# A two-layer graph attention kernel: the last element's finishes cut into 13 pieces without GpSimd's additions, two maxima per beat, and its predecessor's layer 1 at 1.3 steps per beat

## The chip, the cores and the metric

The kernel runs on one core of one Trainium2 chip. The metric is device time in microseconds, of one execution. Engines are named as the profile names them: PE is TensorE's matmul, PEld its weight load, DVE is VectorE, ACT is ScalarE, POOL is GpSimd, SP is SyncE, whose queue issues the DMAs.

## What is computed

There are B = 8 elements of N = 2048 nodes with F = 256 features, and one adjacency matrix for all. Layer 0 is attention with 4 heads, whose softmax is taken over chunks of 256 keys separately; layer 1 is a graph attention layer. Each has a residual and a layer norm.

```
# layer 0
scores = clip(q @ k.T / 8, -10, 10);  scores = where(mask == 0, -10, scores)
attn = softmax(scores, within each of 8 chunks of 256 keys)
y = layernorm(sum over chunks(attn @ v) @ Wo.T + bo + x) * gamma + beta
x = layernorm(x + y)
# layer 1
Wh = x @ W;  s_i = Wh @ a1;  s_j = Wh @ a2
e = leaky_relu(s_i[:, None] + s_j[None, :], 0.2), -inf without an edge
x = layernorm(x + elu(softmax(e) @ Wh))
```

## The kernel before, in words

**Tiles.** Queries go in blocks of IB = 512 (NIB = 4 per element), keys in tiles of 128 (NT = 16) for layer 1 and chunks of 256 (NCH = 8) for layer 0. Everything is fp32, but for the masks.

**Beats.** The order of instructions on each engine is written out by hand: the program emits them in beats. There are 512 beats with scores (8 elements x 4 blocks x 16 key tiles), then a tail of beats without, until the queues of work are empty. Elements and beats are counted from 0 here. Beside the scores, a beat carries layer-1 steps of an earlier element, and one stage of each generator in two lists, `ahead` (the preludes of layer 1) and `fins` (the finishes of blocks). `begin_beat` adds a rate to a credit, and each whole credit starts a layer-1 step: RATE is 1.5 while scores of elements 0 to 6 are made, LAST_RATE (L717) is 1.1 while those of element 7 are, which are the beats that do layer 1 of element 6; in the tail it is 1.0.

**A layer-1 step** (`Step`, 16 per block) makes one key tile's weights for 512 queries in four instructions over four stages: `low` (L642, ACT, 128x512), `leaky` (L646, DVE), `edges` (L651, DVE, with the mask), `weights` (L655, ACT, exponential), and then `product`, four matmuls into PSUM (L674; for the last element L689, with a column of ones that gives the row sums). For elements 0 to 6 GpSimd adds up the weights (L664), whose column sums are the row sums. The tiles w have five buffers.

**The finish of a layer-1 block** (`fin1`, L586) is a generator: it loads the residual hr; divides by the row sums (`divided`, L613, four ACT instructions; for the last element it is called in `product` at once, after two reciprocals, L704); takes the exponential (L601, ACT, 128x1024); the ELU (L603, DVE, 128x1024); adds hr (L604, GpSimd, 128x1024); then statistics (`stats`, L316 and L317, four times each, DVE; L321; and a power -0.5 on GpSimd, L322), `normalize` (L327 on DVE, then four ACT scalings, L329), and stores 512 KB. The finish of a block is emitted in the beats of the next block's steps.

**The finish of a layer-0 block** (`fin`, L342) projects the context (L357), adds, takes statistics, normalizes, multiplies by gamma and adds the residual on GpSimd (L369, L370), takes statistics again, normalizes, stores to h_d, transposes (L382).

**The prelude of the last element** (`last_prelude`, L516). Layer 1 needs for each query the maximum over its neighbours' s_j. `half_max` (L437, one DVE instruction of 128x1024) does one query tile against one half of the keys: 32 in all, `half(it, hf)`. First halves (16) need the far masks in fb tiles, which have two buffers and are loaded one by one, each when a maximum has freed one. One such maximum goes per beat until the last block of layer 0 is finished ("hT"); what is left then is done at once. Masks of the second halves are held in eight tiles loaded together in the third tail beat (L560, 4 MB); the second halves need a row of s_j (L420) that comes out of the last layer-0 block.

**The tail**, in beats: 512 to 520 end layer 0 of the last block; 521 has the remaining first halves and the first four second halves; in 522 to 532 element 6's layer 1 ends; the last element's four blocks of 16 steps follow, each with the finish of the block before; then the last finish alone, to beat 601.

Of the kernel before, what the change touches and what calls it, by code (L numbers as in the profile page):

```python
# [9 lines left out]
F32 = mybir.dt.float32  # L10
# [9 lines left out]
P = 128  # L20
# [8 lines left out]
def tile_adj_attention__then__gat(  # L29
# [312 lines left out]
    def fin(b, ib, ctxT):  # L342


        xt = one.tile([P, TPB, F], F32, tag="x", name=f"x{b}_{ib}")
        nc.sync.dma_start(out=xt, in_=x[b, ts(ib, IB), :].rearrange("(t p) f -> p t f", p=P))
        yield
        y = one.tile([P, TPB, F], F32, tag="y", name=f"y{b}_{ib}")
        nc.gpsimd.tensor_add(y, xt, bc_rows(bo_bc))
        nc.gpsimd.tensor_add(xt, xt, bc_rows(beta_bc))  # L350
        while (b, ib) not in ctx_done or ctx_done[b, ib] == beat:
            yield
        for t2 in range(TPB // 2):
# [12 lines left out]
        yield  # L366
        normalize(y, mv, rstd, f"a{b}_{ib}")
        yield
        nc.gpsimd.tensor_mul(y, y, bc_rows(gamma_bc))  # L369
        nc.gpsimd.tensor_add(y, y, xt)  # L370
        yield
        mv, rstd = yield from stats(y, f"b{b}_{ib}")
        yield
        normalize(y, mv, rstd, f"b{b}_{ib}")
        nc.sync.dma_start(out=h_d[b, ib], in_=y)
        fin_near[b] += 1
        yield
# [138 lines left out]
    def last_prelude(b):  # L516

        st = states[b]  # L520
        wh, rows = [None] * NIB, [None] * 2
        halves = [slice(0, HT), slice(HT, NT)]
        sj = None
        for ib in range(NIB - 1):

            while fin_near[b] <= ib or beat < 2 * total - 12 + 4 * ib:
                yield
            ht = load_hT(b, ib)
            yield
# [12 lines left out]
        m2 = one.tile([P, NIB, 2, TPB], F32, tag="m2l", name=f"m2{b}")  # L542
        firsts = list(range(NT))
        held = None

        def half(it, hf):
            fb = fbs.pop(0) if hf == 0 else held[it // 2][:, ts(it % 2, HN)]
            half_max(rows[hf], fb, m2[:, it // TPB, hf, it % TPB : it % TPB + 1])
            if hf == 0:
                fb_load()  # L550

        while "hT" not in st:
            if firsts:
# [12 lines left out]
        nc.vector.memset(wh[-1][:, :, F : F + 1], 1.0)  # L566
        rows[1] = one.tile([P, HN], F32, tag="v1", name=f"sj_row{b}_1")
        key_rows(b, sj, rows[1], halves[1])
        st["wh"], st["sj"] = wh, sj
        yield  # L570
        while firsts:
            half(firsts.pop(0), 0)
        for ib in range(NIB):
            for t in range(TPB):
                half(ib * TPB + t, 1)
                if ib:
                    yield
            less_max(sj, ib, m2[:, ib], f"{b}_{ib}")
            ab_d = query_rows(m2[:, ib], f"{b}_{ib}")
            yield  # L580

            while blocks_done < b * NIB + ib - 1:
                yield
            st["ab"][ib] = (beat + 1, query_bc(ab_d, f"{b}_{ib}"))

    def fin1(b, ib, hx, acc):  # L586

        hr = one.tile([P, TPB, F], F32, tag="hr", name=f"hr{b}_{ib}")
        nc.sync.dma_start(out=hr, in_=h_d[b, ib])
        yield  # L590


        if acc is not None:
            pr = ps_m.tile([P, TPB], F32, tag="m", name=f"pr{b}_{ib}")
            for t in range(TPB):
                nc.tensor.matmul(pr[:, t : t + 1], acc[:, ts(t, P)], ones[:, 0:1], start=True, stop=True)
            r = two.tile([P, TPB], F32, tag="r1", name=f"r1{b}_{ib}")
            nc.vector.reciprocal(r, pr)
            divided(hx, [hx[:, t, :] for t in range(TPB)], r)
# [3 lines left out]
        nc.vector.scalar_tensor_tensor(hx, ex, 1.0, hx, ALU.min, ALU.max)  # L603
        nc.gpsimd.tensor_add(hx, hx, hr)  # L604
# [4 lines left out]
        nc.sync.dma_start(out=out[b, ts(ib, IB), :].rearrange("(t p) f -> p t f", p=P), in_=hx)  # L609

    def divided(hx, us, r):
        for t in range(TPB):
            nc.scalar.activation(hx[:, t, :], us[t], AF.Identity, bias=ones[:, 0:1], scale=r[:, t : t + 1])  # L613

    states = [{"ab": {}} for _ in range(B)]
    total = B * NIB * NCH
# [15 lines left out]
    class Step:  # L632
# [33 lines left out]
        def product(self):  # L666
# [28 lines left out]
                    )  # L695
            if last:
                blocks_done += 1
                hx = one.tile([P, TPB, F], F32, tag="hx", name=f"hx{self.name}")
# [7 lines left out]
                fins.append(fin1(k["b"], k["ib"], hx, k.get("acc")))  # L706

# [43 lines left out]
    def end_beat():  # L751

        nonlocal weighted
        if beat < 2 * NIB * NCH:
            for fn in agenda.pop(beat, []):
                fn()
        for s in weighted:
            s.product()
        weighted = []
        for gens in (ahead, fins) if beat < 2 * total else (fins, ahead):  # L760
            for g in list(gens):
                if next(g, g) is g:
                    gens.remove(g)
        for fn in agenda.pop(beat, []):
            fn()
# [178 lines left out]
```

## Time and profile before

| | |
|---|---|
| Time, median of 3 runs | 4405.71 us (4405.65 to 4411.56) |
| Profiled execution | 4405.8 us, its span 4404.0 us |
| Mean granted clock of TensorE | 0.979 |
| Busy: PE, PEld | 4064.3 us (92%), 1911.1 us (43%) |
| Busy: DVE, ACT, POOL | 3424.3 (78%), 2567.6 (58%), 1775.2 (40%) |
| L646, leaky, 128x512 | 512 times, mean 1145 ns; 966 ns after 4100 us |
| L651, edges, 128x512 | 512 times, mean 937 ns; 863 ns after 4100 us |
| L437, one maximum with fb, 128x1024 | 240 times, mean 1628 ns |
| L604, residual addition, 128x1024 | 32 times, mean 2856 ns |

A line of the timeline gives start, duration, engine, source line, operation, out<-in, shapes and count; brackets at its end hold the idle time of the engine before it and what ended it. A row of a table by stretches gives the stretch, its length, and each engine's busy time in it with the number of instructions, then the granted clock (1.00 is full), the share of the DMA engines and GB/s. Busy time of PE is of pipelined matmuls, and their ends are modelled.

### The profile page before, as it was taken

How to read it: one execution, taken by the hardware profiler on the slowest of the kernel's cores; microseconds unless marked ns; L12 is line 12 of the kernel's file. 1: busy time of each engine (PE TensorE's matmuls, PEld its weight loads, DVE VectorE, ACT ScalarE, POOL GpSimd, SP SyncE). 2: the span in 40 equal slices, each digit the busy share in tenths (PEclk: the TensorE clock that was granted, in tenths of full speed). 3: DMA queues.
4: the chain of work that ended last, by engine and by line, in shares of the span. 5: the costliest groups of instructions: out<-in, count | busy, mean ns of one | idle time of the engine just before them, and what ended most of it. 6: DMA issues, size and time to landing. Idle time of an engine off the chain costs nothing. (4 is left out here: it accounts for less than half of the span.)

```text
span 4404.0 us, 61164 instructions
## 1 busy us (share of the span) xinstructions
PE 4064.3 (92%) x23053; PEld 1911.1 (43%) x23053; DVE 3424.3 (78%) x4506; ACT 2567.6 (58%) x3846; POOL 1775.2 (40%) x906
## 2 busy tenths in 40 slices
PE   8889999999899999999899998999989999899667
PEld 3223334454344534454344543445434454344355
DVE  5876489965898669976699767996589965897786
ACT  5655456665566556666566665666556665565455
POOL 0222235543455334444245442554335543344421
PEclk9999999999999999999999999999999999999888
DMA  5554232222322233321333223222232222332311
GB/s 165 172 173 147 71 114 85 83 73 87 101 90 80 64 107 102 100 75 50 106 100 97 73 79 101 87 90 78 71 109 90 82 74 85 102 100 71 132 58 48
DMA packets 257625, 415.63 MB, mean 94 GB/s; under 512 B 85424, under 2 KB 120496, under 8 KB 256432
## 3 DMA queue, kind: packets, MB, share of 16 engines
q1 hardware_dynamic: 257328, 411.71, 30.2%
q8 instruction: 181, 2.97, 0.3%
q14 instruction: 116, 0.95, 0.1%
HBM read 340.66 MB, written 68.88 MB: 93 GB/s over the span
## 5 line engine op out<-in xcount | busy, mean ns | idle before, releaser
L821 ACT ACTIVATE e<-sc 128x1024 f32<-128x1024 f32 x1024 | 1034.3, 1020 | 1048.2 <-DVE sc L818 1004.8
L818 DVE SCALAR_TENSOR_TENSOR sc<-sc,mk 128x1024 f32<-128x1024 f32 x1024 | 1206.8, 1223 | 528.0 <-PE sc L808 342.3
L808 PE MATMUL sc<-qT,kT 64*128 64x512 f32 x4096 | 1059.5, 632 | 91.7 <-ACT e L821 91.5
L873 POOL TENSOR_TENSOR ctxT<-ctxT,un 128x1024 f32<-128x1024 f32 x224 | 567.4, 2533 | 1135.1 <-DVE un L872 1021.7
L837 PE MATMUL u<-e,v 128*32 128x512 f32 x8192 | 981.1, 597 | 0.0
L674 PE MATMUL us<-wh,w 128*128 128x256 f32 x3584 | 876.8, 394 | 67.7 <-ACT w L655 50.0
L674 PEld LDWEIGHTS us<-wh,w 128*128 128x128 f32 x3584 | 666.5, 193 | 408.9 <-ACT w L655 99.6
L664 POOL TENSOR_TENSOR acc<-acc,w 128x512 f32<-128x512 f32 x392 | 601.9, 1535 | 553.4 <-ACT w L655 535.0
L808 PEld LDWEIGHTS sc<-qT,kT 64*128 64x128 f32 x4096 | 346.2, 188 | 616.8 <-ACT e L821 286.9
L646 DVE SCALAR_TENSOR_TENSOR w<-ab,sj,w 128x512 f32<-128x512 f32 x512 | 576.1, 1145 | 16.4 <-ACT w L642 16.2
L837 PEld LDWEIGHTS u<-e,v 128*32 128x32 f32 x8192 | 240.7, 110 | 660.5 <-issue 545.9
L651 DVE TENSOR_TENSOR w<-w,mk 128x512 f32<-128x512 f32 x512 | 469.5, 937 | 33.7 <-DMA mk<-mask 30.8
L837 PE MATMUL u<-e,ones 128*32 128x512 f32 x4096 | 495.1, 601 | 0.0
L437 DVE CUSTOM_DVE_ANT_0 fb<-sj_row,fb 128x1024 bf16<-128x1024 f32 x240 | 388.7, 1628 | 7.8 <-DMA fb<-far 7.7
L642 ACT ACTIVATE w<-ab,sj 128x512 f32<-128x512 f32 x512 | 353.3, 715 | 19.9 <-PE us L689 12.7
L655 ACT ACTIVATE w<-w 128x512 f32<-128x512 f32 x512 | 309.3, 628 | 71.5 <-DVE w L651 70.4
L845 ACT COPY un<-u 128x512 f32<-128x512 f32 x512 | 300.6, 587 | 66.9 <-PE u L837 58.2
L872 DVE TENSOR_TENSOR un<-un,r 128x1024 f32<-128x1024 f32 x224 | 280.5, 1252 | 44.1 <-DMA r<-rd 39.0
L837 PEld LDWEIGHTS u<-e,ones 128*32 128x32 f32 x4096 | 107.6, 110 | 352.7 <-issue 301.2
L859 DVE RECIPROCAL dc<-dc 128x16 f32<-128x16 f32 x256 | 63.8, 249 | 147.7 <-DMA dc<-ds 132.0
L604 POOL TENSOR_TENSOR hx<-hx,hr 128x1024 f32<-128x1024 f32 x32 | 91.4, 2856 | 175.2 <-DVE hx L603 175.2
L689 PE MATMUL us<-wh,w 128*128 128x257 f32 x512 | 127.5, 412 | 30.3 <-ACT w L655 30.3
(100 smaller groups left out, 3135.3 us busy)
## 6 DMA issues: line engine op xcount, KB each, us to landing
r<-rd SPq DMA_DIRECT2D x256, 256.0 KB
mk<-mask SPq DMA_DIRECT2D x120, 512.0 KB
fb<-far SPq DMA_DIRECT2D x240, 256.0 KB
xT_k<-in_xT_dram SPq DMA_DIRECT2D x32, 512.0 KB
raw<-in_adjT_dram SPq DMA_DIRECT2D x32, 512.0 KB
rawf<-in_adj_dram SPq DMA_DIRECT2D x32, 512.0 KB
x<-in_x_dram SPq DMA_DIRECT2D x32, 512.0 KB
h_d<-y SPq DMA_DIRECT2D x32, 512.0 KB
```

The source lines that it names most:

```text
L437: nc.vector.tensor_tensor_reduce(out=fb, in0=row, in1=fb, scale=1.0, scalar=2 * FAR * 0.999, op0=ALU.add, op1=ALU.max, accum_out=dst,)
L642: nc.scalar.activation(self.w, k["ab"][:, 1, :], AF.Identity, bias=k["sj"][:, 1, c : c + 1])
L646: nc.vector.scalar_tensor_tensor(self.w, k["ab"][:, 0, :], k["sj"][:, 0, c : c + 1], self.w, ALU.add, ALU.max)
L651: nc.vector.tensor_tensor(self.w, self.w, self.k["mks"][self.c // HT][:, self.c % HT, :], ALU.min)
L655: nc.scalar.activation(self.w, self.w, AF.Exp)
L664: nc.gpsimd.tensor_add(k["acc"], k["acc"], self.w)
L674: nc.tensor.matmul(k["us"][:, t, :], self.w[:, ts(t, P)], k["wh"][c // TPB][:, c % TPB, 0:F], start=(first and t % 2 == 0), stop=last, ski ...
L808: nc.tensor.matmul(sc[:, h, :], kTs[b][c // TPB][h * D : (h + 1) * D, hp, ts(c % TPB, P)], qT[h * D : (h + 1) * D, hp, :], start=True, sto ...
L818: nc.vector.scalar_tensor_tensor(scs[hp], scs[hp], -CLIP, cap, ALU.max, ALU.min)
L821: nc.scalar.activation(e, scs[hp], AF.Exp)
L837: nc.tensor.matmul(m[h * DH : (h + 1) * DH, :], prev["v"][pc // TPB][:, pc % TPB, f0 : f0 + DH] if part < 2 else ones[:, 0:DH], prev["es"] ...
L873: nc.gpsimd.tensor_add(p["ctxT"], p["ctxT"], p["un"])
```

## The change

- LAST_RATE is 1.3 in place of 1.1.
- In the tail, two first-half maxima are emitted per beat in place of one, as long as there are any; the agenda (the scaling of layer-0 contexts) runs at the front of the beat's end there, too.
- The layer-0 finish of the very last block multiplies by gamma and adds the residual on DVE.
- For the last element, `fin1` is replaced by `fin1_last`. Of the four divisions, two go to DVE. The finish of blocks 0, 1, 2 has 13 pieces, one per beat: two exponentials of half the block, two ELUs, two additions on DVE, four tiles of statistics, the spread (with the power on GpSimd), two pairs of scalings, then the store. The finish of block 3 is emitted in one go, half after half, each with its own spread and store.
- Blocks 1 and 3 of the last element use the buffer of y for hx.

```diff
@@ in fin
-        nc.gpsimd.tensor_mul(y, y, bc_rows(gamma_bc))
-        nc.gpsimd.tensor_add(y, y, xt)
+        engine = nc.vector if (b, ib) == (B - 1, NIB - 1) else nc.gpsimd
+        engine.tensor_mul(y, y, bc_rows(gamma_bc))
+        engine.tensor_add(y, y, xt)
@@ in last_prelude
-            if firsts:
-                half(firsts.pop(0), 0)
+            for it in firsts[: 2 if beat > 2 * total else 1]:
+                half(it, 0)
+                firsts.remove(it)
@@ new
+    def fin1_last(b, ib, hx):
+        hr = one.tile([P, TPB, F], F32, tag="hr", name=f"hr{b}_{ib}")
+        nc.sync.dma_start(out=hr, in_=h_d[b, ib])
...
+        def exponential(r):
+            nc.scalar.activation(ex[:, r, :], hx[:, r, :], AF.Exp, bias=shifts[:, 1:2])
+        def elu(r):
+            nc.vector.scalar_tensor_tensor(hx[:, r, :], ex[:, r, :], 1.0, hx[:, r, :], ALU.min, ALU.max)
+        def add(r):
+            nc.vector.tensor_add(hx[:, r, :], hx[:, r, :], hr[:, r, :])
+        def tile_stats(t):
+            nc.vector.bn_stats(st[:, t, :], hx[:, t, :])
+            nc.vector.bn_aggr(mv[:, t, :], st[:, t, :])
+        def spread_of(r):
+            nc.vector.tensor_scalar_add(rstd[:, r], mv[:, r, 1], EPS)
+            nc.gpsimd.tensor_tensor(rstd[:, r], rstd[:, r], nhalf[:, r], ALU.pow)
+            nc.vector.scalar_tensor_tensor(nmr[:, r], mv[:, r, 0], -1.0, rstd[:, r], ALU.mult, ALU.mult)
...
+        halves = [slice(0, 2), slice(2, 4)]
+        if ends:
+            for r in halves:
+                exponential(r)
+            for r in halves:
+                elu(r)
+                add(r)
+                for t in range(r.start, r.stop):
+                    tile_stats(t)
+                spread_of(r)
+                for t in range(r.start, r.stop):
+                    scale(t)
+                store(r)
+            return
+        yield
+        for r in halves:
+            exponential(r)
+            yield
+            elu(r)
+        yield
+        for r in halves:
+            add(r)
+            yield
         for t in range(TPB):
+            tile_stats(t)
+            yield
+        spread_of(slice(0, TPB))
+        yield
+        for r in halves:
+            for t in range(r.start, r.stop):
+                scale(t)
+            yield
+        store(slice(0, TPB))
@@ in product, at the last key tile
+                tag = "y" if k["b"] == B - 1 and k["ib"] % 2 else "hx"
...
-                    divided(hx, [k["us"][t // 2][:, t % 2, 0:F] for t in range(TPB)], r)
+                    for t in (0, 2):
+                        nc.scalar.activation(
+                            hx[:, t, :],
+                            k["us"][t // 2][:, t % 2, 0:F],
...
+                        nc.vector.tensor_scalar(
+                            hx[:, t + 1, :],
+                            k["us"][t // 2][:, t % 2 + 1, 0:F],
...
+                    fins.append(fin1_last(k["b"], k["ib"], hx))
+                    return
@@
-    RATE, LAST_RATE = 1.5, 1.1
+    RATE, LAST_RATE = 1.5, 1.3
@@ in end_beat
-        if beat < 2 * NIB * NCH:
+        if beat < 2 * NIB * NCH or beat >= 2 * total:
             for fn in agenda.pop(beat, []):
                 fn()
```

More of the change, by code (lines that the diff above doesn't have):

```diff
@@ L590, in fin1 @@
         yield
[L593 to L599, printed above, removed]
+        pr = ps_m.tile([P, TPB], F32, tag="m", name=f"pr{b}_{ib}")
+        for t in range(TPB):
+            nc.tensor.matmul(pr[:, t : t + 1], acc[:, ts(t, P)], ones[:, 0:1], start=True, stop=True)
+        r = two.tile([P, TPB], F32, tag="r1", name=f"r1{b}_{ib}")
+        nc.vector.reciprocal(r, pr)
+        for t in range(TPB):
+            nc.scalar.activation(hx[:, t, :], hx[:, t, :], AF.Identity, bias=ones[:, 0:1], scale=r[:, t : t + 1])
         ex = one.tile([P, TPB, F], F32, tag="ex", name=f"ex{b}_{ib}")
@@ L609, in fin1, with scale, store @@
         nc.sync.dma_start(out=out[b, ts(ib, IB), :].rearrange("(t p) f -> p t f", p=P), in_=hx)
-    def divided(hx, us, r):
-        for t in range(TPB):
-            nc.scalar.activation(hx[:, t, :], us[t], AF.Identity, bias=ones[:, 0:1], scale=r[:, t : t + 1])
+    def fin1_last(b, ib, hx):
+        hr = one.tile([P, TPB, F], F32, tag="hr", name=f"hr{b}_{ib}")
+        nc.sync.dma_start(out=hr, in_=h_d[b, ib])
+        ex = one.tile([P, TPB, F], F32, tag="ex", name=f"ex{b}_{ib}")
+        st = two.tile([P, TPB, 6], F32, tag="st", name=f"st_c{b}_{ib}")
+        mv = two.tile([P, TPB, 2], F32, tag="mv", name=f"mv_c{b}_{ib}")
+        rstd = two.tile([P, TPB], F32, tag="rstd", name=f"rstd_c{b}_{ib}")
+        nmr = two.tile([P, TPB], F32, tag="nmr", name=f"nmr_c{b}_{ib}")
+        ends = ib == NIB - 1
+        def exponential(r):
[11 more added lines that the diff above has]
+            nc.vector.scalar_tensor_tensor(nmr[:, r], mv[:, r, 0], -1.0, rstd[:, r], ALU.mult, ALU.mult)
+        def scale(t):
+            nc.scalar.activation(
+                hx[:, t, :], hx[:, t, :], AF.Identity, bias=nmr[:, t : t + 1], scale=rstd[:, t : t + 1]
+            )
+        def store(r):
+            n = (r.stop - r.start) * P
+            q0 = ib * IB + r.start * P
+            nc.sync.dma_start(out=out[b, q0 : q0 + n, :].rearrange("(t p) f -> p t f", p=P), in_=hx[:, r, :])
+        halves = [slice(0, 2), slice(2, 4)]
[21 more added lines that the diff above has]
+            yield
+        for t in range(TPB):
+            tile_stats(t)
[7 more added lines that the diff above has]
+        store(slice(0, TPB))
@@ L697, in product @@
                 blocks_done += 1
-                hx = one.tile([P, TPB, F], F32, tag="hx", name=f"hx{self.name}")
+                tag = "y" if k["b"] == B - 1 and k["ib"] % 2 else "hx"
+                hx = one.tile([P, TPB, F], F32, tag=tag, name=f"hx{self.name}")
                 if k["b"] < B - 1:
@@ L704, in product @@
                         nc.vector.reciprocal(r[:, ts(n, 2)], k["us"][n][:, :, F])
[L705 to L706 removed]
+                    for t in (0, 2):
+                        nc.scalar.activation(
+                            hx[:, t, :],
+                            k["us"][t // 2][:, t % 2, 0:F],
+                            AF.Identity,
+                            bias=ones[:, 0:1],
+                            scale=r[:, t : t + 1],
+                        )
+                        nc.vector.tensor_scalar(
+                            hx[:, t + 1, :],
+                            k["us"][t // 2][:, t % 2 + 1, 0:F],
+                            r[:, t + 1 : t + 2],
+                            1.0,
+                            ALU.mult,
+                            ALU.add,
+                        )
+                    fins.append(fin1_last(k["b"], k["ib"], hx))
+                    return
+                fins.append(fin1(k["b"], k["ib"], hx, k["acc"]))
     l1 = layer1()
```

## The prediction

> **What bounds the kernel now.** I read the page's 40 slices first: the tensor engine is at 9 tenths nearly everywhere and falls to 6 to 7 in the last three. So the end is another stage than the rest, and I cut the last 604 us into stretches. Columns: stretch, length, busy us of PE, PEld, DVE, ACT, POOL (instructions), granted clock, DMA share, GB/s.
>
> ```profile
> core 0: us, PE busy (x) PEld busy (x) DVE busy (x) ACT busy (x) POOL busy (x), PEclk, DMA share, GB/s
> 3800.00:4100.00 300.00, 284.18 (x1667) 131.09 (x1666) 253.22 (x333) 179.07 (x273) 139.61 (x70) 1.00 0.29 89
> 4100.00:4168.00 68.00, 43.40 (x186) 30.81 (x185) 59.18 (x83) 27.54 (x49) 42.79 (x22) 0.82 0.41 143
> 4168.00:4190.00 22.00, 1.17 (x7) 0.69 (x5) 14.39 (x29) 2.08 (x4) 0.67 (x1) 0.59 0.35 108
> ...
> 4207.00:4222.00 15.00, 12.85 (x49) 10.20 (x49) 14.38 (x15) 8.08 (x15) 9.48 (x6) 0.89 0.29 100
> ...
> 4269.00:4310.00 41.00, 31.95 (x128) 25.80 (x128) 33.38 (x58) 24.33 (x42) 5.12 (x2) 0.92 0.19 65
> 4310.00:4348.00 38.00, 30.48 (x131) 25.26 (x130) 28.25 (x45) 24.64 (x42) 4.20 (x2) 0.96 0.15 56
> 4348.00:4388.00 40.00, 32.32 (x131) 26.20 (x129) 26.98 (x44) 23.76 (x41) 4.18 (x2) 0.91 0.08 27
> 4388.00:4404.00 16.00, 0.00 (x0) 0.00 (x0) 3.69 (x12) 4.36 (x8) 3.35 (x2) 0.57 0.10 33
> ```
>
> To 4100 (scores and layer 1 together) PE is busy 284.2 of 300 us: PE bounds it, 15.8 us idle, DVE next with 253.2. After it PE is busy 43.4 of 68, 1.2 of 22, 12.9 of 15, then 32.0 of 41, 30.5 of 38, 32.3 of 40 in the last element's three later blocks, and DVE is never full there either. These are hand-overs. The timeline of the border before the last block names them (start, length, engine, line; in brackets the idle time before it and who ended it):
>
> ```profile
> 4353.68 2.73 POOL L604 TENSOR_TENSOR hx<-hx,hr 128x1024 f32<-128x1024 f32 x1 [30.65 <-DVE hx L603]
> 4354.24 2.72 DVE L651 TENSOR_TENSOR w<-w,mk 128x512 f32<-128x512 f32 x1
> ...
> 4361.07 2.07 ACT L329 ACTIVATE hx<-hx,nmr_c,rstd_c 128x256 f32<-128x256 f32 x4 [2.83 <-DVE nmr_c L327]
> ...
> 4363.71 24.12 PE L689 MATMUL us<-wh,w 128*128 128x257 f32 x96 [4.03 <-ACT w L655]
> ...
> 4365.70 0.74 DVE L646 SCALAR_TENSOR_TENSOR w<-ab,sj,w 128x512 f32<-128x512 f32 x1
> ...
> 4367.09 0.75 DVE L646 SCALAR_TENSOR_TENSOR w<-ab,sj,w 128x512 f32<-128x512 f32 x1
> ...
> 4374.05 0.72 ACT L642 ACTIVATE w<-ab,sj 128x512 f32<-128x512 f32 x1 [0.49 <-PE us L689]
> ...
> 4375.79 0.72 ACT L642 ACTIVATE w<-ab,sj 128x512 f32<-128x512 f32 x1 [0.49 <-PE us L689]
> ...
> 4399.97 0.39 SPq L609 DMA_DIRECT2D out_dram<-hx  x1
> ```
>
> The GpSimd addition (L604) runs from 4353.68 to 4356.41, and the 0.69 us DVE instruction L651 under it takes 2.72. Statistics and power follow; ScalarE reaches L329 and waits 2.83 for nmr, does four scalings (2.07), and only then the exponential that PE needs: PE idles 4.03. The next four lines give two paces: DVE alone does a step (L646 and L651) in 4367.09 - 4365.70 = 1.39 us; PE sets 4375.79 - 4374.05 = 1.74 per step. The wait has a second price, seen in the clock:
>
> ```profile
> 4364.00:4366.00 2.00, 2.00 (x5) 1.56 (x6) 1.66 (x3) 1.59 (x4) 0.00 (x0) 0.50 0.97 287
> ...
> 4368.00:4370.00 2.00, 2.00 (x6) 1.54 (x6) 1.93 (x3) 1.08 (x2) 0.00 (x0) 0.53 0.00 0
> 4372.00:4376.00 4.00, 4.00 (x21) 3.49 (x20) 3.39 (x6) 2.69 (x5) 0.00 (x0) 1.00 0.00 0
> ```
>
> For 6 us from 4364 the granted clock is 0.50 to 0.53, so PE loses some 3 us more. Of the waits from 4100 on, one bears on the maxima (us in total, times, longest):
>
> ```profile
> DVE fb L437 <- DMA fb<-far: 7.5, 3, 4.0
> ```
>
> **What the Trainium skill says.** "SBUF — State Buffer", Who interferes with whom: VectorE and GpSimd share one port pair as an exclusive lock, and a DVE instruction with two SBUF inputs contends with a GpSimd one that reads SBUF. The trace agrees (0.69 to 2.72 above; L646 from 0.75 to 2.82 at 4276.57 under the 3.20 us L604). "TensorE: Matmul & The Clock Gate", What's actually happening: after an idle window of about 3.4 us the clock is halved until it has been busy about as long. The trace agrees in kind (0.50 after 4.03 us). "GPSIMD Engine Reference", Performance versus the Vector engine: an elementwise addition takes 1.96 times as long as on VectorE; here 2.34 to 3.33 us for 128x1024 against 1.22. "VectorE: DVE Perf Modes", Why PSUM operands drop a tier: a PSUM operand in fp32 has only the 1x mode; so for the new 128x256 division on DVE I use the 1x row of that size, bn_stats, 0.40 us. No trace shows that operation.
>
> **The change part by part.** Beats are counted in program order from 0; scores end with beat 511. What each beat holds comes from following both programs' order; times from the trace of before.
>
> A. LAST_RATE 1.1 to 1.3. At beat 512 before has begun step 11 of element 6's third block, after step 1 of its fourth: 6 steps earlier. They move into the stretch to 4100, which PE bounds: 6 x 1.75 (steady pace 1.74, 1.93 when alone in the chain) = +10.5 us. At least +3 if they fill half of the 15.8 idle us; at most +15, if DVE sets the pace there (0.75 + 0.69 and one lock of about 1.0).
>
> D. What that buys. Beats 527 to 532 vanish: before they run from the L646 at 4207.03 to the one at 4221.31, -14.3 us. They are dear since each has a GpSimd accumulation that locks DVE (L646 1.76, L651 1.64).
>
> B. Two maxima per beat. In 513 to 519 seven more maxima: 7 x 1.15 (distance of L437 starts) = +8.1, less 1.0 for the wait on the output projection (3.0 us at 4129.96) that one of them fills. The two fb buffers are loaded only when a maximum is done, so a pair can wait: before, the three waits above (3.97, 1.91, 1.59), with nothing between the pairs. Now 1.4 us or more of steps and finishing lie between, and in most beats 3.7 us; the 8 held loads (12.8 us of transfer) are behind 14 us of beat 515. I take +2 (0 to 10). In beat 521 the seven leftover maxima go: before from 4166.1 to 4189.8 = 23.7. After: the row of the second half, hidden so far, comes bare (issued 4167.76, its packets end about 4170.4, ready 4170.7, so 4.6), then 4 x 1.15 and the small maxima 0.8: 10.0. -13.7. Together -4.6.
>
> C. The last layer-0 finish multiplies and adds on DVE: +2.44 (2 x 1.22); GpSimd loses 2.79 + 2.68. DVE's wait for it (2.24, at 4148.64) and one lock (2.03) go: -1.8.
>
> E. The finishes of blocks 0, 1, 2 in 13 pieces, beside the steps of blocks 1, 2, 3. DVE per block after the change, from PE's end of the block before: reciprocal and two divisions 1.1; 15 steps x 1.395 = 20.9; four halves of ELU and addition 4 x 0.61 = 2.4; four statistics 2.2; small ones with the wait for the power on GpSimd 1.4 (1.3 at the end of before); then ScalarE's exponential 0.75 and PE's last step 1.95: 30.7, say 30.9. PE alone needs 1.4 + 16 x 1.74 = 29.2, so DVE becomes the bound by a little, PE never idles 3.4 us and the clock stays. ScalarE's scalings stand behind the exponential and the nmr they wait for is two DVE instructions before the next edges, so its 1.04 us pairs are covered; uncovered they cost at most 1 per beat. Before, from PE end to PE end (4269.1, 4310.7, 4348.5, 4387.8): 41.5, 37.8, 39.4. Block 1 keeps four maxima and small ones: 30.9 + 4.6 + 0.8 = 36.2. Savings 5.3, 6.9, 8.5 = -20.7. Bounds: -27 at PE's pace, -10 if the pieces hand over badly. The store moves behind the next steps on SP: the mask load of the next block (512 KB) stands behind it, and still has four DVE steps, 5.6 us, against about 4; at no cost, with up to 2 per block if it is late. hr of the last block is queued behind a store too, some 8 us ahead of need.
>
> F. The last finish in halves. Before: PE end to store issue 4399.97 - 4387.83 = 12.1. After: divisions end +1.0, exponential of half one +1.4, ELU, addition, two statistics +3.8, power and nmr +5.35 (DVE waits there), second half the same +9.25, scaling +10.4. -1.7; and the last store has half the bytes (its 512 KB took about 1.5 us), -0.75: -2.5.
>
> Tags, the merged division and running the agenda ahead in the tail: no instruction more, 0; the agenda only puts ctxT's additions ahead of others on GpSimd.
>
> Sum: 10.5 - 14.3 - 4.6 - 1.8 - 20.7 - 2.5 = -33.4. The profiled execution took 4405.8 (span 4404.0 and 1.8 around it), the median is 4405.71: both give 4372.
>
> **The rivals.**
> 1. More: idle time in the main stretch takes most of A (+3) and the blocks reach PE's pace (-6.5): 4372 - 7.5 - 6.5 = 4358. For it: 15.8 idle us. Against: DVE is 0.84 busy there and adds up in the last blocks.
> 2. Less: DVE is the bound in the stretch to 4100 (A +15), maxima wait 5 more, and each piece costs a hand-over so that E gives half: 4372 + 4.5 + 5 + 10.5 = 4392. For it: DVE was busy 47.9 of 50 in 3850 to 3900.
> 3. Slower: the fb loads. If each of the 14 maxima of beats 513 to 519 waits like the longest one, 3.97, this is 55.6 instead of 2: 4426. It decides from (33.4 + 2) / 14 = 2.5 us per maximum. For it: two buffers, and held loads of 4 MB in the same queue. Against: the second and third wait of before were 1.9 and 1.6, with nothing between.
> 4. That the steps don't move or the pieces don't spread is out: the order shows both.
>
> **How the numbers follow.** Forecast 4372 (4362 to 4383): 0.60. Rival 1 (below 4362): 0.14. Rival 2 (4383 to 4397): 0.16. Within 0.2% (8.8 us, about what a measurement of this kernel can tell from no change): 0.06, two shortfalls together. Slower: 0.04. Range 4356 to 4391: all of the forecast, most of rival 1, more than half of rival 2. Faster 0.90, same 0.06, slower 0.04.
>
> **What would show it.** Right: scores end about 10 us later; 14 us less between there and the last element's first step, beside the 6 us of B and C; later blocks some 31 us apart (36 for the one with maxima) with clock 1.00; no GpSimd addition and no 2.7 us DVE instruction in them; end 2.5 us shorter. Wrong: waits of the maxima on fb loads over 10 us; PE idle over 3 us at a border; scores ending over 16 us later.

## The result, and the profile after

The changed kernel took 4395.03 us, median of 7 runs (4387.29 to 4401.29), against 4405.71 before: ratio 0.9968, 95% interval 0.9957 to 0.998. The forecast was 4372, range 4356 to 4391. The direction was right, and a third of the gain came. The profiled execution took 4387.29 (span 4385.5), the fastest of the seven.

Stretches of the changed kernel, columns as in the prediction's table; they are cut at its own hand-overs:

```profile
3800.00:4100.00 300.00, 278.33 (x1584) 132.07 (x1584) 254.63 (x330) 176.26 (x268) 143.53 (x74) 0.98 0.28 84
4114.00:4179.00 65.00, 37.09 (x156) 25.89 (x154) 61.29 (x86) 22.06 (x37) 36.93 (x18) 0.74 0.53 168
...
4268.00:4307.00 39.00, 32.38 (x129) 26.11 (x129) 32.56 (x63) 24.06 (x41) 1.01 (x1) 0.91 0.20 68
4307.00:4339.50 32.50, 30.21 (x128) 23.37 (x128) 27.56 (x50) 23.86 (x40) 1.01 (x1) 1.00 0.18 65
...
4372.00:4385.50 13.50, 0.12 (x1) 0.00 (x0) 6.60 (x19) 4.09 (x8) 1.39 (x2) 0.59 0.11 39
```

The scores end at 4114 instead of 4100. The first row can't be compared as it stands: it holds more layer-1 steps than before (45 leaky instructions, before 40) and fewer scores (71 clips, before 76). Over the whole of element 7's 64 beats of scores PE is busy 482.7 us instead of 470.6 and idle 37.3 instead of 28.5: of 20.9 us more, 12.1 are busy time and 8.8 idle. Part of the busy time is slow: the granted clock was 0.50 for 17.1 us of these beats, before for 6.8. From 4114 to 4179 DVE is busy 61.3 of 65 us, so it is the busiest engine there. The last three blocks last 39.3, 32.6 and 32.6 us (before 41.5, 37.8, 39.4), GpSimd is busy 1 us in each instead of 4 to 5, and the clock is 1.00 in the last two.

What answers to the border shown of before, and the two paces, in the timeline of the changed kernel:

```profile
4308.29 21.07 PE L761 MATMUL us<-wh,w 128*128 128x257 f32 x88 [1.38 <-DVE hx L787]
...
4319.44 0.72 DVE L718 SCALAR_TENSOR_TENSOR w<-ab,sj,w 128x512 f32<-128x512 f32 x1
...
4321.36 0.72 DVE L718 SCALAR_TENSOR_TENSOR w<-ab,sj,w 128x512 f32<-128x512 f32 x1
...
4327.93 0.16 DVE L641 SCALAR_TENSOR_TENSOR nmr_c<-mv_c,rstd_c 128x4 f32<-128x4 f32 x1 [1.21 <-POOL rstd_c L640]
...
4330.20 9.32 PE L761 MATMUL us<-wh,w 128*128 128x257 f32 x40 [0.84 <-ACT w L727]
```

PE no longer idles 4.03 us at a border but 1.38. No DVE instruction takes 2.7. A step with one piece of the finish takes 4321.36 - 4319.44 = 1.92 on DVE, and PE does 11 steps in 21.07, which is 1.92 each: DVE sets the pace. Then DVE stands 1.21 for GpSimd's power, PE idles 0.84, and the last five steps take 9.32, 1.86 each.

The clock in the first of these blocks, in the columns of the table:

```profile
4282.00:4284.00 2.00, 1.19 (x3) 1.00 (x4) 1.97 (x4) 2.00 (x5) 0.00 (x0) 0.54 0.01 2
...
4286.00:4288.00 2.00, 2.00 (x6) 1.63 (x5) 1.93 (x5) 1.31 (x3) 0.00 (x0) 0.50 0.00 0
...
4290.00:4292.00 2.00, 2.00 (x11) 1.74 (x10) 1.90 (x6) 1.60 (x3) 0.00 (x0) 1.00 0.00 0
```

The waits, and the end:

```profile
DVE fb L438 <- DMA fb<-far: 1.2, 2, 1.0
```

```profile
4376.57 0.69 POOL L640 TENSOR_TENSOR rstd_c<-rstd_c,nhalf 128x2 f32<-128x2 f32 x1 [16.07 <-DVE rstd_c L639]
...
4378.61 4.10 SPq L651 DMA_DIRECT2D out_dram<-hx  x2
```

The maxima wait 1.2 us for their masks in all, before 7.5. The power for half a block takes 0.69, and the row of the stores begins with the first half's at 4378.61; from PE's last end to the end of the span it is 13.4 us, before 16.2.

**A trap in comparing the two traces.** Up to beat 447, the last of element 6's scores, no edit of this study touches the order of instructions. In 18 traces the clip of that beat ends between 3594.0 and 3614.1 us. The trace of after has the lowest of all, 3594.0; before has 3601.2. So 7 us of the profiled difference are no effect of the change, and they hid the loss in the next stretch: scores 13.65 us later in absolute time are 20.9 us more from beat 447 on. All sums below therefore start at that clip. (The clip of a beat is its DVE instruction on the scores, L818 before and L909 in the changed kernel.) From there to the end, before takes 802.8 us, the changed kernel 791.5, and in a second trace of it 790.5: 11.3 to 12.3 us less, as the medians say (10.7).

### The profile page after: what moved, and what is told of

Its sections match the earlier page's. It is cut to its first block, busy times and chain, and to the rows that moved or that the text cites. A ratio compares the mean times of both kernels' runs of the same rounds, so it can differ in the third digit from the quotient of the medians.

```text
span 4385.5 us, 61171 instructions
## 1 busy us (share of the span) xinstructions
PE 4064.2 (93%) x23053; PEld 1907.6 (43%) x23053; DVE 3417.7 (78%) x4530; ACT 2564.4 (58%) x3842; POOL 1760.5 (40%) x901
## 3 DMA queue, kind: packets, MB, share of 16 engines
q1 hardware_dynamic: 257344, 411.71, 30.5%
## 5 line engine op out<-in xcount | busy, mean ns | idle before, releaser
L912 ACT ACTIVATE e<-sc 128x1024 f32<-128x1024 f32 x1024 | 1034.2, 1020 | 1049.9 <-DVE sc L909 1006.7
L909 DVE SCALAR_TENSOR_TENSOR sc<-sc,mk 128x1024 f32<-128x1024 f32 x1024 | 1206.7, 1223 | 538.3 <-PE sc L899 352.6
L746 PE MATMUL us<-wh,w 128*128 128x256 f32 x3584 | 878.6, 395 | 81.9 <-ACT w L727 60.4
L723 DVE TENSOR_TENSOR w<-w,mk 128x512 f32<-128x512 f32 x512 | 458.6, 917 | 37.1 <-DMA mk<-mask 34.6
L942 ACT COPY ds<-u 128x512 f32<-128x512 f32 x256 | 148.5, 580 | 3.0 <-PE u L928 2.5
L349 POOL TENSOR_TENSOR y<-x,bo_bc 128x1024 f32<-128x1024 f32 x32 | 77.6, 2426 | 163.6 <-DMA x<-in_x_dram 103.0
```

The source lines that it names most:

```text
L723: nc.vector.tensor_tensor(self.w, self.w, self.k["mks"][self.c // HT][:, self.c % HT, :], ALU.min)
L746: nc.tensor.matmul(k["us"][:, t, :], self.w[:, ts(t, P)], k["wh"][c // TPB][:, c % TPB, 0:F], start=(first and t % 2 == 0), stop=last, ski ...
L909: nc.vector.scalar_tensor_tensor(scs[hp], scs[hp], -CLIP, cap, ALU.max, ALU.min)
L912: nc.scalar.activation(e, scs[hp], AF.Exp)
```

## The experiments

Columns: the 64 beats with scores of element 7 (clip of beat 447 to clip of beat 511), from there to the end, their sum, and the ratio to the kernel before. "Nmr to b" is the time from the last clip to nmr of the last layer-0 finish's second norm; blocks are those of the last element from PE end to PE end, block 1 to 3. Each row has one trace; the two traces of the changed kernel agree within 0.4 us in the tail, and 64 beats in the same order lie within 2.5 us of their mean. Each ratio is to the kernel before as measured beside that kernel, whose median lay between 4405.7 and 4411.6; medians of different rows can't be subtracted. Below, the seven traces at 1.3 are those in which that LAST_RATE alone places the steps (changed, again, steps_only, one_max, y_gps, hold62, nofirst13), the eight at 1.1 those with that rate (before, fins_only, rate11, fins_split, best1, best4, nofirst11, no_add).

| kernel | beats 448-511 | tail | sum | nmr to b | blocks 1, 2, 3 | median us | ratio (95%) |
|---|---|---|---|---|---|---|---|
| before | 499.2 | 303.7 | 802.8 | 53.2 | 41.5 37.8 39.4 | 4405.71 | |
| changed | 520.0 | 271.5 | 791.5 | 65.4 | 39.3 32.6 32.6 | 4395.03 | 0.9968 (0.9957-0.998) |
| again | 518.6 | 271.9 | 790.5 | 64.5 | 38.0 32.6 32.6 | 4400.62 | 0.9975 (0.9965-0.9986) |
| fins_only | 500.2 | 285.5 | 785.7 | 53.2 | 38.0 32.6 32.6 | 4391.0 | 0.9957 (0.9944-0.9969) |
| steps_only | 521.0 | 295.9 | 816.9 | 61.4 | 41.9 38.0 37.8 | 4428.26 | 1.0036 (1.0023-1.0048) |
| one_max | 516.9 | 274.9 | 791.8 | 55.3 | 38.0 32.6 32.6 | 4398.38 | 0.9975 (0.9968-0.9981) |
| y_gps | 520.3 | 275.0 | 795.3 | 67.3 | 38.0 32.6 32.6 | 4399.06 | 0.9971 (0.996-0.9983) |
| rate11 | 500.6 | 278.2 | 778.8 | 58.9 | 38.0 32.6 32.6 | 4384.96 | 0.994 (0.9928-0.9953) |
| late_steps | 513.2 | 274.8 | 788.0 | 68.0 | 38.0 32.6 32.6 | 4390.49 | 0.9954 (0.9943-0.9966) |
| nopair | 512.2 | 276.9 | 789.0 | 68.0 | 37.9 32.6 32.6 | 4395.18 | 0.9978 (0.9968-0.9988) |
| hold62 | 519.7 | 265.3 | 785.0 | 59.9 | 38.0 32.6 32.6 | 4396.8 | 0.9958 (0.9945-0.9971) |
| fins_split | 502.8 | 284.0 | 786.8 | 52.0 | 38.0 31.6 31.9 | 4390.14 | 0.9953 (0.9941-0.9965) |
| best1 | 501.2 | 275.7 | 777.0 | 59.3 | 38.0 31.6 31.8 | 4389.59 | 0.9946 (0.9932-0.9959) |
| best3 | 511.2 | 263.2 | 774.4 | 59.5 | 37.7 31.6 31.9 | 4380.86 | 0.9942 (0.993-0.9955) |
| best4 | 499.4 | 293.4 | 792.8 | 60.7 | 38.0 31.6 31.9 | 4398.1 | 0.9977 (0.9968-0.9986) |

**again.** The changed kernel unaltered.

> The changed kernel once more, unaltered. Its seven times lay between 4387.3 and 4401.3 us, in groups near 4388 and 4396, while the kernel before lay between 4404.9 and 4411.6. Theory: the groups differ by one or two losses of TensorE's clock (each some 3 us of half clock at a hand-over), so this run's profiled execution shows either the same span as the first (4385.5) within 1 us or one of 4393 to 4399 whose difference sits in single stretches where the granted clock is lower. Rival: the difference is spread over the whole run (many small waits on transfers), so no stretch of 300 us shows more than 2 us of it.

The span was 4390.7. Its tail agrees with the first trace within 0.4 us and the 64 beats within 1.4; the clip of beat 447 ends 6.2 us later. Neither of the spans that the theory named came. The 6.2 us pile up before beat 447, in pieces of up to 3.0 us per 32 beats, in the part that all kernels share (over 18 traces the clip of beat 31 already ends between 218.6 and 224.6 us), so no clock loss in the tail makes them. But the clock varies there, too: before the clip of beat 447 it was 0.50 for 64.8 to 102.4 us in the 18 traces, and the longer it was, the later that clip ended (correlation 0.73; in the 14 pieces of 32 beats 0.38 to 0.93). The pieces in which this trace falls behind the first by 2.9 and 2.4 us (beats 192 to 223 and 256 to 287) have 6.8 and 3.4 us more at 0.50; in both traces the total is 81.9 us, so it is not all. What starts a loss in one execution and not in the other stays open.

**fins_only, steps_only.** The two halves of the change, each on the kernel before.

```diff
 fins_only: fin1_last, its tags and divisions as in the change; nothing else
 steps_only:
-    RATE, LAST_RATE = 1.5, 1.1
+    RATE, LAST_RATE = 1.5, 1.3
```

> The kernel before with the new finishes of the last element alone (parts E and F): LAST_RATE 1.1, one maximum per beat, gamma and residual of the last layer-0 finish on GpSimd, agenda as before. Theory from the two traces: all of the gain in the profiled execution lies here. Blocks 1, 2, 3 from 41.5, 37.8, 39.4 us to about 39, 32.6, 32.6, the end 2.8 shorter: -17, so 4389 us, with the end of the first element's product before it unchanged at 4224 (within 1 us). Rival, the forecast's sizes: blocks of 36.2, 30.9, 30.9 and the end 2.5 shorter, -23, so 4383 us.

> The kernel before with LAST_RATE 1.3 in place of 1.1 and nothing else (parts A and D). Theory from the two traces: the six steps cost 2.3 us each ahead of the end of the scores (13.7 us), and the six beats that vanish give 14.3 back: -0.6, no change, 4405 us, scores ending near 4114. Rival, the forecast: the six steps cost TensorE's pace, 1.75 each (10.5), so -3.8, 4402 us, scores ending near 4111. A third way: beats 513 to 521 are no shorter but DVE is freer, and 3 us or more are lost or won there; then the stretch from the end of the scores to beat 522 differs from 89.4 us of before.

The finishes give 18.2 us in the tail, near the theory and short of the forecast's 23. The steps alone make the kernel 14.1 us slower, which neither theory nor rival expected: the 64 beats take 21.9 more, the tail only 7.8 less. The third way did come: from the last clip to the first step of beat 522 it is 95.7 us instead of 89.4. The gain of D was halved, the cost of A doubled.

**one_max, y_gps.** B and C undone, at 1.3.

```diff
 one_max:
-            for it in firsts[: 2 if beat > 2 * total else 1]:
+            for it in firsts[:1]:
 y_gps:
-        engine = nc.vector if (b, ib) == (B - 1, NIB - 1) else nc.gpsimd
+        engine = nc.gpsimd
```

> The changed kernel with one maximum per beat again (part B undone). Theory from the two traces: the maxima only changed places; beats 512 to 520 grew by 12.4 us and beat 521 shrank by 12.9, so undoing it leaves the time within 2 us, 512 to 520 near 68 us and 521 near 23.5. Rival, the forecast: B is worth 4.6 us, so 4.6 us slower. Third: the pairs of maxima cost more than they give, since DVE is the engine that sets the pace in 512 to 520 and the row of the second half then comes bare; then it is 3 us or more faster.

> The changed kernel with gamma and the residual of the very last layer-0 finish on GpSimd again (C undone). Forecast: C is worth 1.8, so the tail after the last score is 1.8 longer. Rival, from the trace of the changed kernel: DVE sets the pace there, and its two instructions took 2.30 and 2.17 us beside GpSimd's accumulations instead of 1.22 each, so undoing C makes the tail some 2 us shorter (269.5 instead of 271.5 to 271.9).

Read in the tail, against 271.7 (mean of the two traces of the changed kernel), B is worth 3.2 and C 3.3. The theory for one_max (within 2 us) was wrong, too. The forecast's signs hold; that their sum, 6.5, is its 6.4 is luck, since each is off by 1.4 or more. My reading of the locked 2.30 and 2.17 us was wrong: GpSimd's own pair costs the chain more.

**rate11, late_steps.** A and D undone; then the same six steps moved, but later.

```diff
 rate11:
-    RATE, LAST_RATE = 1.5, 1.3
+    RATE, LAST_RATE = 1.5, 1.1
 late_steps, on top of rate11:
-            begin_beat(RATE if b < B - 1 else LAST_RATE)
+            begin_beat(RATE if b < B - 1 else LAST_RATE if beat < 490 else 1.4)
```

> The changed kernel with LAST_RATE 1.1 again (A and D undone; B, C, E, F stay). Theory after the first runs: element 7's 64 beats of scores are 19 to 21 us longer at 1.3, not 10.5, and the tail is 14.3 shorter. Undone: 500 us for these beats instead of 519, the tail 14.3 longer, so about 5 us faster than the changed kernel in the 800 us from the last beat of element 6 on (near 786). Rival, the forecast's sizes: A costs 10.5 and D gives 14.3, so 3.8 us slower.

> The changed kernel with the same six steps moved ahead of the end of the scores, but all of them later: 1.1 steps per beat up to beat 489, 1.4 from 490 on. Theory: a moved step costs TensorE's 1.75 us, and the other 10 us of the 20 come from the place where the border of element 6's first block falls (beats 486 to 491, beside maxima, statistics and GpSimd's multiplications). With the border where it was, the 64 beats take 500 + 10.5 = 511 us instead of 519, the tail is unchanged: 8 us faster than the changed kernel. Rival: DVE is the bound and each step costs 3.3 us wherever it lies: 519, no gain.

At 1.1 the sum is 778.8: 12.2 us better than the changed kernel, more than expected, since the tail loses only 6.5 instead of 14.3. Moved late, six steps cost 12.6 us (513.2 - 500.6) instead of 18.7 (mean of changed and again, 519.3), near the 10.5 of the theory. So the place matters: beats 486 to 491 take 45.3 to 48.6 us in the eight traces at 1.1 and 56.1 to 57.3 in the seven at 1.3, 9.9 of a mean difference of 18.4; in late_steps they take 50.2. The tail of late_steps was expected unchanged and is 3.1 us longer, so its sum is 3.0 better than the changed kernel's and not 8: the third block's last product falls in beat 513 there and its finish meets the last layer-0 finish (nmr at 68.0; see hold62).

**nofirst13, nofirst11.** No maximum of element 7 before the tail, at 1.3 and at 1.1.

```diff
-            for it in firsts[: 2 if beat > 2 * total else 1]:
+            for it in firsts[: 2 if beat > 2 * total else 0]:
```

> The changed kernel (1.3 steps per beat) with no first-half maximum before the tail: all 16 are made in beats 513 to 520. Only the 64 beats with scores of element 7 are read, beside the same kernel at 1.1. Theory: the maxima are what fills DVE there (0.84 to 0.95 busy), and the six steps cost 19.4 us instead of 10.5 because they push DVE over its limit; without the maxima the 64 beats at 1.3 are 10 to 12 us longer than at 1.1. Rival: the place of the block's border and GpSimd's locks do it, and the difference stays over 16 us.

> The same at 1.1 steps per beat, the partner of the run at 1.3. Both theories expect the 64 beats to be shorter than the 500.6 us with maxima, if DVE's maxima cost anything there at all; if they cost nothing at 1.1 (PE sets the pace), 499 to 501.

519.2 and 503.5 us (4391.87 and 4395.02 us in one run each). The edits change nothing in these beats: only two of the 16 first halves stand before beat 513 at all, both behind the last clip. The maxima seen in beats 486 to 491 are of element 6's own prelude. So the pair tells nothing of DVE; it repeats the 64 beats at 1.3 (516.9 to 521.0 in seven traces) and at 1.1 (499.2 to 503.5 in eight).

**nopair.** In beat 487 the changed kernel issues both the last product of element 6's first block and the first of its second. The timeline of the changed kernel there:

```profile
3887.99 2.71 POOL L371 TENSOR_TENSOR y<-y,x 128x1024 f32<-128x1024 f32 x1
3888.38 3.40 DVE L438 CUSTOM_DVE_ANT_0 fb<-sj_row,fb 128x1024 bf16<-128x1024 f32 x1
...
3901.83 2.00 PE L746 MATMUL us<-wh,w 128*128 128x256 f32 x8
...
3902.86 2.36 DVE L909 SCALAR_TENSOR_TENSOR sc<-sc,mk 128x1024 f32<-128x1024 f32 x2
...
3904.12 2.15 ACT L912 ACTIVATE e<-sc 128x1024 f32<-128x1024 f32 x2 [4.06 <-DVE sc L909]
...
3906.63 1.03 ACT L773 COPY hx<-us 128x1024 f32<-128x1024 f32 x1
...
3907.72 3.78 PE L746 MATMUL us<-wh,w 128*128 128x256 f32 x8 [3.89 <-ACT hx L773]
```

The second product (3907.72) goes to the same PSUM tile and waits 3.89 us for ScalarE's copy L773 (3906.63). The copy stands behind the exponentials L912, which waited 4.06 for DVE's clips L909. DVE is late there; that the maximum at 3888.38 took 3.40 under GpSimd's addition (3887.99, L371) is part of it. It is as late without the pair: in rate11 the exponentials of the same beat wait 5.06 us. After the wait the same eight matmuls take 3.78 instead of 2.00 us: the granted clock was 0.50 for 6.83 us from 3906.7. In beats 486 to 491 all seven traces at 1.3 have 6.8 or 10.2 us at 0.50, the eight at 1.1 none.

```diff
                 lows.append(s)
                 s.low()
+                if s.k["b"] == B - 2 and s.c == NT - 1:
+                    break
```

> The changed kernel (1.3) with one rule more: of element 6, no step starts in the beat in which a block's last step has started, so the last product of a block and the first of the next never stand in one beat. Theory: in beat 487 both stood together, the second waited 3.9 us for ScalarE's copy out of PSUM, which stood behind exponentials that waited for DVE. Parted, the 64 beats with scores take 511 to 514 us with 5 steps ahead of the kernel at 1.1 instead of 518.6 to 520.3 with 6, beats 486 to 491 some 6 us less than in the changed kernel. Rival: TensorE's wait only moves to another instruction, since DVE is late there anyway: 517 or more (the one step fewer is worth 1.75).

In the timeline of nopair the copy has a beat's scores beside it:

```profile
3908.49 2.26 PE L901 MATMUL sc<-qT,kT 64*128 64x512 f32 x8 [2.85 <-ACT e L914]
...
3909.93 1.03 ACT L773 COPY hx<-us 128x1024 f32<-128x1024 f32 x1
...
3914.67 1.56 PE L746 MATMUL us<-wh,w 128*128 128x256 f32 x6 [0.35 <-ACT w L727]
```

PE still waits for exponentials (2.85, and 1.51 a beat earlier), so DVE is late with or without the pair, but the copy is over before the product needs it (0.35), and no matmul of these beats runs at half clock (in best3, in the same order, the clock is 0.50 for 3.4 us). Beats 486 to 491 take 49.1 instead of 57.0 us, the 64 beats 512.2: 7.2 us less than the mean at 1.3 (519.4), and best3, 511.2, repeats it. The rule starts one step fewer by beat 511, which at the forecast's price would be 1.75 us: up to the last clip PE does as many products as in the changed kernel, five more than before, and DVE one leaky less. So the theory holds in these beats. In the whole kernel it doesn't show: nopair's tail is 5.2 us longer, its sum only 2.0 better, its ratio no better than the changed kernel's. The third block's last product falls in beat 513, as in late_steps, and nmr comes at 68.0; in best3, which holds that finish, the tail is 263.2 and the gain stays.

**hold62.** The finish of element 6's third block begins in beat 517 again.

```diff
     def fin1(b, ib, hx, acc):
+        while (b, ib) == (B - 2, NIB - 2) and beat < 2 * total + 5:
+            yield
```

> The changed kernel with one thing moved: the finish of element 6's third block (whose last product now falls in beat 512, before in 517) begins in beat 517, as in the kernel before. Theory: at 1.3 the tail is only 7 us shorter than at 1.1 though the six vanished beats were worth 14.3, because this finish came to lie among the last layer-0 finish of beats 512 to 520 and delays it (nmr of its second norm comes 64.5 to 65.4 us after the last score, 58.9 at 1.1). Held, nmr comes at 59 and the tail falls from 271.7 to about 264.5 us. Rival: it is the steps or the maxima themselves, and the tail stays within 2 us of 271.7.

Of the changed kernel, the timeline of beats 513 to 519, that finish's instructions and what they hold up:

```profile
4137.80 1.21 DVE L605 SCALAR_TENSOR_TENSOR hx<-ex,hx 128x1024 f32<-128x1024 f32 x1
...
4141.18 3.33 POOL L606 TENSOR_TENSOR hx<-hx,hr 128x1024 f32<-128x1024 f32 x1
...
4142.23 3.36 DVE L438 CUSTOM_DVE_ANT_0 fb<-sj_row,fb 128x1024 bf16<-128x1024 f32 x1
...
4161.55 2.06 ACT L329 ACTIVATE hx<-hx,nmr_c,rstd_c 128x256 f32<-128x256 f32 x4
...
4179.45 0.15 DVE L327 SCALAR_TENSOR_TENSOR nmr_b<-mv_b,rstd_b 128x4 f32<-128x4 f32 x1
```

Its addition on GpSimd (L606, 3.33 us) locks maxima (3.36 for the one at 4142.23), its statistics and ELU stand on DVE, its scalings on ScalarE ahead of the next step's exponential; nmr_b comes at 4179.45. In hold62 its ELU stands just behind nmr_b:

```profile
4181.81 0.16 DVE L327 SCALAR_TENSOR_TENSOR nmr_b<-mv_b,rstd_b 128x4 f32<-128x4 f32 x1
4181.88 1.22 DVE L607 SCALAR_TENSOR_TENSOR hx<-ex,hx 128x1024 f32<-128x1024 f32 x1
...
4184.19 3.33 POOL L608 TENSOR_TENSOR hx<-hx,hr 128x1024 f32<-128x1024 f32 x1
```

The last clip of hold62 is at 4121.9, so nmr_b comes 59.9 us after it, and the tail is 265.3. That is near the theory's 59 and 264.5: that finish took 6.4 of the 14.3 us back.

**fins_split, no_add.** What sets the pace of the last blocks.

```diff
 fins_split, on fins_only (spread_of without its last instruction):
         spread_of(slice(0, TPB))
         yield
+        shift_of(slice(0, TPB))
+        yield
 no_add, on best1:
         for r in halves:
-            add(r)
             yield
```

> The kernel before with the new finishes alone, and in these the instruction that waits for GpSimd's power (nmr, DVE) one piece later than the power, so in 14 pieces. DVE then does a step in between instead of standing idle for 1.1 to 1.2 us per block. Theory: in blocks 1, 2, 3 DVE sets the pace, so each is 0.8 to 1.2 us shorter: tail near 283 instead of 285.45, a gain of 2.5 us on the kernel with the new finishes alone. Rival: ScalarE's scalings move beside the exponentials of the last steps and the wait only changes its name: within 0.5 us.

> The kernel at LAST_RATE 1.1 with nmr one piece after the power, and without the residual additions of the last element's blocks 0, 1 and 2 (left out of the computation: x is not added to the ELU there), 2 x 0.61 us less of DVE's work in each of blocks 1, 2, 3. Theory: DVE sets the pace of blocks 2 and 3 and they go from 31.6 to 30.4; block 1 is set by TensorE's clock and stays at 38.0 (within 0.5), or gains as much if DVE's chain ahead of its idle time sets it. Rival: TensorE's front wait and pace set blocks 2 and 3, and they lose under 0.4.

no_add leaves out the residual additions of the last element's blocks 0, 1 and 2 (one run, 4383.98 us). With nmr a piece later DVE stands 0.17 us for the power instead of 1.21, as the timeline of fins_split shows:

```profile
4331.39 0.16 DVE L639 TENSOR_SCALAR rstd_c<-mv_c 128x4 f32<-128x4 f32 x1
4331.46 0.74 DVE L723 SCALAR_TENSOR_TENSOR w<-ab,sj,w 128x512 f32<-128x512 f32 x1
...
4333.11 0.16 DVE L643 SCALAR_TENSOR_TENSOR nmr_c<-mv_c,rstd_c 128x4 f32<-128x4 f32 x1 [0.17 <-POOL rstd_c L640]
```

Blocks 2 and 3 go from 32.6 to 31.6 and 31.9; block 1 stays at 38.0; the tail is 1.5 us shorter, not 2.5. Without 1.22 us of additions they go from 31.6 and 31.8 to 30.4 and 30.5, in full: DVE sets their pace. Block 1 gains 0.6 only.

**best1, best3, best4.** best1 is rate11 with the split. best3 is the changed kernel with nopair, hold62 and the split. best4 is best1 with that finish held to beat 521 (`2 * total + 9`).

> The changed kernel at LAST_RATE 1.1 with nmr one piece after the power. Theory: the two add up, the tail goes from 278.2 to 276.5 us, the time from the last beat of element 6 on from 778.8 to about 777, the median near 4383. Rival: within 0.5 us of the kernel at 1.1 alone in the tail.

> The changed kernel at 1.3 with the two products parted, the finish of element 6's third block held to beat 517, and nmr one piece after the power. Theory: the gains add up: 512 for the 64 beats, tail 265.3 - 1.7 + 1 or 2 for the one beat more, so 777 to 779 us from the last beat of element 6 on, level with the kernel at 1.1 (777.0 with the same finishes). Rival: 785 or more, if parting the products gives nothing.

> The kernel at LAST_RATE 1.1 with nmr one piece after the power, and the finish of element 6's third block held from beat 517 to 521. Theory: at 1.1 that finish still meets the last layer-0 finish in beats 517 to 520 (nmr of its second norm 58.9 to 59.3 us after the last score); held, it comes 1 to 4 us earlier and the tail falls from 275.7 to 272 to 275. Rival: the finish then meets the maxima of beat 521 and the steps of 522 to 527, and the tail is not shorter than 275.7.

In the sum, best1 and best3 add up as expected, best3 better by some 3 us (best1's median, expected near 4383, is 4389.59). At 4380.86 best3 has the lowest median of the study, but its ratio is level with those of rate11 and best1. best4 failed: nmr_b comes no earlier (60.7), and element 6's last product ends 133.0 us after the last clip instead of 116.2 in best1. Held that long, the finish falls among the steps of beats 522 to 533, as the rival said; which of its instructions delays them stays open.

## Why the forecast was wrong, point by point

| step | forecast | measured | from |
|---|---|---|---|
| A, six steps ahead | +10.5 | +18.4 | 64 beats: mean of the seven traces at 1.3 (519.4) less that of the eight at 1.1 (501.0) |
| D, beats vanish | -14.3 | -6.5 | rate11 to the changed kernel, tails |
| B, two maxima | -4.6 | -3.2 | one_max, tail |
| C, gamma on DVE | -1.8 | -3.3 | y_gps, tail |
| E, 13 pieces | -20.7 | -15.6 | three blocks, before to again |
| F, halves | -2.5 | -2.8 | PE end to span end |
| sum | -33.4 | -13.0 | measured from beat 447: -11.3 and -12.3 |

That the direction was right is owed to E and F (-18.4) and to B and C (-6.5). A and D together, the change of LAST_RATE, were forecast at -3.8 and cost 11.9: at 1.1 the kernel is better (ratio 0.994 against 0.9968 and 0.9975).

**A failed**: "6 x 1.75 (steady pace 1.74, 1.93 when alone in the chain) = +10.5 us", with "at most +15". It priced a step as PE's work and asked how much of it fits into idle time, not where the block's border would fall. In beat 487 the products of two steps of different blocks came to stand together, at a place where DVE was late already, and the wait cost the clock, too. nopair and best3 show this: parted, the 64 beats are 7.2 and 8.2 us shorter, of which one step fewer started would be 1.75 at the forecast's price; the excess is 7.9. What else there is was not isolated: beats 502 and 503 take 4.8 to 5.5 us more both in the changed kernel and in nopair, beats 504 to 511 take 3.2 less in the changed kernel.

**D failed**: "Beats 527 to 532 vanish: ... -14.3 us." They did vanish, and their price was nearly right (hold62: -12.9 against rate11). From the last clip to the last element's first product it was 125.4 us before and is 111.1, 14.3 less, where D, B and C promised 20.7 together. Moving steps moves what hangs on them: the third block's border went from beat 517 to 512 and took its finish (an addition of 3.33 us on GpSimd, some 4 us of work on DVE, 5 on ScalarE) into the chain of the last layer-0 finish. That a step's finish moves with it was nowhere in the sum.

**E was mis-sized**: the mechanism is right in blocks 2 and 3 (no addition on GpSimd, no lock, DVE the bound), the sum "30.7, say 30.9" is not: they took 32.6. (Two small slips: 30.9 + 4.6 + 0.8 is 36.3 and not 36.2, and the bound of -27 at PE's pace doesn't follow from its 29.2 per block, which with the 5.4 of block 1 gives -25.7.) It took the larger of two totals, 30.7 for DVE and 29.2 for PE. The bounds follow each other within a block: 1.38 of front wait, 11 steps at DVE's 1.92, 0.84 of idle, then five steps where DVE could do 1.39 and PE needs 1.74 to 1.86; together 1.38 + 21.07 + 0.84 + 9.32 = 32.6. And "PE never idles 3.4 us and the clock stays" fails in block 1: PE idled 1.82 and 0.88 us with 0.27 of work between, and the clock went to 0.50 for 6.8 us. All 16 traces with the new finishes have such a loss in block 1 (3.4 us in the other 15: 22.76 us for the 12 steps in rate11, 24.10 here, 20.9 at full clock), none in blocks 2 and 3. The Trainium skill, "TensorE: Matmul & The Clock Gate", What's actually happening, names an idle window of about 3.4 us; no single idle time here is longer than 1.82, so the measurement decides: less is enough. In no_add the two are 1.21 and 0.88, and the clock still goes to 0.50. Whether these two alone do it, or also the four waits ahead of them in the block (1.38, 1.19, 0.53, 1.14), isn't separated; a wait of 1.38 at the border is followed by no loss in blocks 2 and 3.

**B, C and F** came near. The lock that B's maxima meet agrees with the skill's "SBUF — State Buffer", Who interferes with whom (a DVE instruction with two inputs in SBUF beside a GpSimd one that reads SBUF), and is larger than the forecast's 1.0 us: a maximum takes 1.22 us alone, 3.36 under L606. Rival 2 landed nearest in time (4392), which is luck, since its reasons were others: A was more than its +15, the maxima waited less and not more, and E gave three quarters and not half. Rival 3 is out: 1.2 us of waits on fb.

## What to carry to other kernels

When a rate moves steps earlier in an order that is written out by hand, list first which beats the borders land in, which finishes move with them, and whether the last product of one tile and the first of the next now share a beat; here these cost more than the steps. Where two engines are near each other's pace, add up a block phase by phase, and don't take the larger of two totals. Compare traces from a point that the change can't have touched.

## What was not expected of the hardware

- The granted clock went to 0.50 after idle times of 1.82 and 0.88 us (in no_add 1.21 and 0.88), none of which is long. With the same idle times in 15 traces the loss begins between 14.5 and 16.0 us after PE's end of the block before, and lasts 3.41 us in 14 of them and 6.83 in one.
- The power -0.5 on GpSimd takes 1.01 us for 128x4 and 0.69 to 0.70 for 128x2; beside a multiplication or a maximum on DVE 1.9 to 2.0, beside its statistics 1.02.
- The division of 128x256 out of PSUM takes DVE 0.48 us; the forecast took 0.40 from bn_stats of that size.
- The same sequence of instructions, 3.6 ms long, ended anywhere within 20 us in 18 traces, while beats 504 to 511 took 63.73 or 63.74 us in the seven traces at 1.3.
